# A y-major copy of the queries for the position logits of a two-layer attention kernel

## The chip, the cores and the metric

The kernel runs on one core of one Trainium2 chip. The metric is device time in microseconds (us) of one execution, the median of three runs. The core has a matrix engine (TensorE, PE in the profile; its weight loads are listed apart as PEld), a vector engine (VectorE, DVE), a scalar engine (ScalarE, ACT), a general engine (GpSimd, POOL) and a queue engine that starts transfers (SyncE, SP). Each works through its own instructions in their order and waits for the others through semaphores. Operands lie in on-chip memory of 128 partitions; matmul results go to banks of a separate accumulator memory.

## The reference

The input x has 8 images of 32 x 32 positions with 512 channels. Two layers follow, each of the form x + attention(group norm of x). All arithmetic is float32.

- Layer 0: 16 heads of 32 channels. q, k, v are products of the normed image with one weight matrix; softmax of q k / sqrt(32) over the 1024 positions, times v, then an output projection with a bias.
- Layer 1: 4 heads of 128 channels, three weight matrices for q, k, v and one for the output. Before the softmax a relative position logit is added. For a query at row x and column y and a key at row x' and column y' it is

```
rel_w = einsum('bhxyd,dr->bhxyr', q_w, pos_emb_w)   # entry r picked by y' - y
rel_h = einsum('bhyxd,dr->bhyxr', q_h, pos_emb_h)   # entry r picked by x' - x
scores = attn_q @ k + rel_w + rel_h
```

So for every query column y the queries of that column (all 32 rows, 4 heads) are multiplied with 32 columns of pos_emb_w that depend on y, and for every query row x with 32 columns of pos_emb_h that depend on x.

## The kernel before

Everything of one image is kept channel-major: a block is a tile of 128 partitions (channels of a chunk) by 4 chunks by 1024 positions. The pool has 8 blocks (BLOCKS, line 24). Position n of an image is 32 x + y, so the queries of one row x are 32 adjacent floats and those of one column y are 32 floats apart.

**Products.** Every 512 x 512 projection is done by a Strassen-Winograd scheme of seven products on half matrices, in two units (`seven`, line 417; order of the seven in ORDER, line 181). Each product is a generator step that yields the cost 2 (HC). A unit takes three accumulator banks, x, y and z, from a pool of three ("bank", line 82), which the position logits, and layer 1's scores, use too. ACT copies p1, p7 and the first quarter c11 out of the banks. DVE adds a, b and the quarters c12 and c21. POOL adds the fourth quarter, c22.

**Layer 0's attention** (`attention_0`, line 714) runs through 64 steps per image. A step makes the scores of four heads in a 4-bank tile ps of its own (line 727), lets ACT take the exponential of 128 x 2048 values (line 742, into one of three slots of e_room), multiplies the previous step's exponentials with v (line 753) and lets DVE add them up (line 765).

**Layer 1's attention** (`attention_1`, line 840) adds the position logits by a matmul of posT with a fixed selection matrix (line 851).

**Position logits** (`position_logits`, line 797) are made in four tiles pp per image, each in one bank. A tile holds eight columns y and eight rows x. Line 811 multiplies the queries of one column, line 818 those of one row, each a 128 x 32 weight and 4 x 32 moving columns, on four column strips of the matrix engine. A float32 matmul appears as two records in the trace. From each tile ACT casts four parts of 32 partitions into posT (line 831), rounded to the short matmul format, and DVE writes what the rounding lost into the other partitions (line 836).

**Order.** The program is written by generators. `woven(main, side, start, gap, places)` (line 1151) takes a step of the side after those main steps whose number minus start, modulo gap, is in places. `side_by_side` (line 1163) runs the 64 steps of layer 0's attention of image b and puts beside them, by the yielded costs, all other work: the output projections of earlier images, layer 1's q, k, v and position logits of image b-1 (`second`, line 1083), layer 1's attention of b-1 in one piece (its steps cost 0), and the projections for image b+1. A position tile yields -2, so another product follows before the next attention step. After image 7's layer 0 attention the rest of image 7 runs alone.

A scheduler then orders the instructions of each engine by this program order and by when it expects their operands; `tc.issue_after(ins)` makes what is written inside come after `ins` on its engine. A block or bank is given to a new tile when all users of the old one are done.

In `second`, the q projection runs first, with two sums of the normed image beside it. Then the k projection and the v projection run, 28 products, with the position logits beside them from product 2 on: a tile after products 2, 9, 16 and 23, and its two pairs of differences after the two products that follow.

Of the kernel before, what the change touches and what calls it, by code (L numbers as in the profile page):

```python
# [12 lines left out]
AF = mybir.ActivationFunctionType  # L13
# [14 lines left out]
def quick_path(  # L28
# [23 lines left out]
    nc = tc.nc  # L52

    B, IH, IW, C = x.shape
# [3 lines left out]
    NB = 512  # L58
    NH = N // NB
    D0 = 32  # L60
# [14 lines left out]
    def block(name, shape=None, dtype=F32):  # L75
        return mem.tile(shape or [P, CC, N], dtype, tag="block", name=name, bufs=BLOCKS)

    def chunks(block):
        return [block[:, i, :] for i in range(CC)]
# [51 lines left out]
    HC, HN = CC // 2, NB // 2  # L131
# [49 lines left out]
    ORDER = [0, 5, 1, 4, 6, 2, 3]  # L181
# [151 lines left out]
    beside_norm = [False]  # L333

    added = [None]

    def by_columns(out, weights, moving, start, stop, open_sum=False):

        for g in range(P // 32):
            columns = slice(32 * g, 32 * g + 32)  # L340
            ins = nc.tensor.matmul(  # L341
                out[columns, :],
                weights[:, columns],
                moving,
                start=start,
                stop=stop,
                skip_group_check=open_sum,
            )
            if in_place[0]:
                tc.keep_in_program_order(ins)  # L350
        in_place[0] = False
# [286 lines left out]
    def project_T(fs, m, y, name, units=(0, 1)):  # L638

        for u in units:  # L640
            stream.unit(m, False, u)
            yield from seven(fs, u, False, Plain(halves(y, u)), f"{name}_{u}")
# [71 lines left out]
    def attention_0(q, k, v, b, blocks=range(NT)):  # L714

        steps = [(m, h, j) for m in (0, 2, 1, 3) for h in range(NH) for j in blocks]
        state = {}

        def front(m, h, j):
            name = f"0_{b}_{m}_{h}_{j}"  # L720
            ps = psum.tile([P, HB, NB], F32, tag="ps", name=f"ps_{name}", bufs=1)
            for i in range(2):

                some = slice(64 * i, 64 * i + 64)
                for r in range(HB):
                    rows = slice(r * D0, (r + 1) * D0)
                    nc.tensor.matmul(  # L727
                        ps[some, r, :],
                        k[m][rows, j * P + 64 * i : j * P + 64 * i + 64],
                        q[m][rows, h * NB : (h + 1) * NB],  # L730
                        start=True,
                        stop=True,
                    )
            at = turn.pop(0)
            if j == blocks[0]:

                turn.append(sum_at[0])
                sum_at[0] = at
            else:
                turn.append(at)  # L740
            e = e_room[:, at]
            nc.scalar.activation(e, ps, AF.Exp, scale=D0 ** -0.5)  # L742
            return e

        def back(m, h, j, e):
            name = f"0_{b}_{m}_{h}_{j}"
            if j == blocks[0]:
                state["acc"] = psum.tile([P, NB], F32, tag="acc", name=f"acc_{name}", bufs=1)
                state["first"] = e
            acc = state["acc"]  # L750
            for r in range(HB):
                c0 = (m * HB + r) * D0
                nc.tensor.matmul(  # L753
                    acc[r * D0 : (r + 1) * D0, :],
                    v[:, j, c0 : c0 + D0],
                    e[:, r, :],
                    start=(j == blocks[0]),
                    stop=(j == blocks[-1]),
                )
            if j == blocks[1]:  # L760
                state["esum"] = state["first"]
            if j != blocks[0]:

                with tc.issue_after(reader[0].ins) if beside_norm[0] else nullcontext():
                    summed[0] = nc.vector.tensor_add(state["esum"], state["esum"], e)  # L765
            if j != blocks[-1]:
                return
            nc.scalar.copy(q[m][:, h * NB : (h + 1) * NB], acc)
            state["ended"] = (m, h, state["esum"])

        def finish(m, h, esum):
            name = f"0_{b}_{m}_{h}"
            su = psum.tile([P, NB], F32, tag="acc", name=f"sums_{name}", bufs=1)
            for r in range(HB):
                nc.tensor.matmul(
                    su[r * D0 : (r + 1) * D0, :],
                    ones,
                    esum[:, r, :],
                    start=True,
                    stop=True,  # L780
                )
            normalise(q[m][:, h * NB : (h + 1) * NB], su, name)

        pending = None
        for at in steps:
            if "ended" in state:
                finish(*state.pop("ended"))
            e = front(*at)
            if pending is not None:
                back(*pending)  # L790
            pending = (*at, e)
            yield 2
        back(*pending)
        yield 1
        finish(*state.pop("ended"))

    def position_logits(q, posT, b):

        qv = q.rearrange("p h (x y) -> p h x y", y=IW)
        by_y = posT.rearrange("p h (x s r) -> p r s h x", r=2, s=IW // 2)
        by_x = posT.rearrange("p h (s r y) -> p r s h y", r=2, s=IH // 2)
        G = NB // (IW * H1)
        for t in range(IW // (2 * G)):
            pp = bank(f"pp_{b}_{t}", [P, G, H1, 32])
            for g in range(G):
                for r in range(2):
                    s = 2 * (t * G + g) + r  # L810
                    nc.tensor.matmul(
                        pp[64 * r : 64 * r + 32, g],
                        pw_sb[:, IW - 1 - s : 2 * IW - 1 - s],
                        qv[:, :, :, s],
                        start=True,
                        stop=True,
                    )
                    nc.tensor.matmul(  # L818
                        pp[64 * r + 32 : 64 * r + 64, g],
                        ph_sb[:, IH - 1 - s : 2 * IH - 1 - s],  # L820
                        qv[:, :, s, :],
                        start=True,
                        stop=True,
                    )
            parts = []
            for r in range(2):
                for u, view in enumerate((by_y, by_x)):
                    view = view[:, r, t * G : (t + 1) * G]
                    rows = slice(64 * r + 32 * u, 64 * r + 32 * u + 32)
                    rests = slice(64 * (1 - r) + 32 * u, 64 * (1 - r) + 32 * u + 32)  # L830
                    nc.scalar.copy(view[rows], pp[rows])  # L831
                    parts.append((view[rests], pp[rows], view[rows].bitcast(F32)))

            yield -2
            for i, (rest, logits, greater) in enumerate(parts):
                nc.vector.tensor_sub(rest, logits, greater)  # L836
                if i % 2:
                    yield 0
# [244 lines left out]
    def second(b, st):  # L1083

        if "xn1" in st:
            fs, sums = st.pop("xn1"), st.pop("sums1")
        else:
            fs, sums = forms(st.pop("x1"), f"xn1_{b}"), iter(())
        q = st["ao"] = block(f"q1_{b}")
        yield from woven(project_T(fs, WQ1, chunks(q), f"q1_{b}"), sums, 0, 2 * len(ORDER), (0, 3))  # L1090
        posT = block(f"posT_{b}", dtype=F32R)
        k = chunks(block(f"k1_{b}"))
        v = block(f"v1_{b}", [P, NT, C])
        keys_and_values = chain(
            project_T(fs, WK1, k, f"k1_{b}"), project_rows(fs, WV1, v, f"v1_{b}")
        )

        yield from woven(
            keys_and_values, position_logits(q, posT, b), 2, len(ORDER), (0, 1, 2)
        )  # L1100
        st["at"] = (q, k, v, posT, b)

    def forms_1(b, st):
# [47 lines left out]
    def woven(main, side, start, gap, places=(0,)):  # L1151

        for at, cost in enumerate(main):
            if at >= start and (at - start) % gap in places:
                cost += next(side, 0)
            yield cost
        yield from side
# [21 lines left out]
    def chain(*parts):  # L1179
        for part in parts:  # L1180
            yield from part
# [20 lines left out]
    WP, WQ1, WK1 = Matrix(w_proj, 0, "p"), Matrix(Wq, 0, "q1"), Matrix(Wk, 0, "k1")  # L1202
# [46 lines left out]
    for b in range(B + 1):  # L1249
        rest, total = [], 0  # L1250
        s = [None] * 2 + states + [None] * 2
# [555 lines left out]
```

## Time and profile before

| quantity | value |
|---|---|
| median of three runs | 3792.49 us (3792.39 to 3792.98) |
| profiled execution, its own time | 3792.3 us |
| its span, first to last instruction | 3790.5 us |
| granted clock of the matrix engine | 0.999 |
| position casts, line 831, ACT | 128, 105.7 us busy, mean 826 ns |
| position differences, line 836, DVE | 128, 111.8 us busy, mean 874 ns |
| exponentials of layer 0, line 742, ACT | 512, 961.9 us busy, mean 1879 ns |
| additions of layer 0, line 765, DVE | 448, 1074.6 us busy, mean 2399 ns |

Busy time of a group is the time in which at least one of its instructions runs. The mean of one matmul record is from its start to its last result; the engine begins the next ones long before, so distances between starts tell more than durations. In a timeline a line gives the start, the length, the engine, the source line and the operation, with neighbours of one kind merged (x16: sixteen records). What follows in brackets is how long the engine was idle before and what it waited for. In a table of windows, each engine's busy time in the window is followed by the number of its instructions.

### The profile page before, as it was taken

The page shows a single profiled execution, that of the slowest core. Times are in us where ns is not written, and L with a number is a line of the kernel's source. Part 1 is how long each engine was busy: PE and PEld are TensorE (multiplying, and loading weights), DVE is VectorE, ACT ScalarE, POOL GpSimd, SP SyncE. Part 2 cuts the span into 40 slices and gives each one's busy share as a digit, 9 for nine tenths or more (in the row PEclk, how much of TensorE's full clock was granted, in tenths as well). Part 3 has the DMA queues.
Part 4 walks back from the last instruction along what each step waited for, and adds up shares of the span by engine and source line. Part 5 has one row for each costly group of instructions (what it writes and reads, how often), then busy time and mean ns, then how long its engine had stood idle before and what let it go on. Part 6 is the DMA issues. An engine that isn't in the chain of part 4 may idle for free. (4 is left out here: it accounts for less than half of the span.)

```text
span 3790.5 us, 79715 instructions
## 1 busy us (share of the span) xinstructions
PE 3764.2 (99%) x34478; PEld 1367.7 (36%) x34478; DVE 2579.9 (68%) x2974; ACT 1689.2 (45%) x1705; POOL 651.4 (17%) x397
## 2 busy tenths in 40 slices
PE   9999999999999999999999999999999999999998
PEld 4232244322443234432343323433234332334353
DVE  6778675686756867569665696656866569765555
ACT  3555543445434454344534445344453445553132
POOL 1342101131001310013101131011310113001201
PEclk9999999999999999999999999999999999999999
DMA  6122120232202312023120241103411033110321
GB/s 187 64 106 69 39 57 10 72 102 54 56 12 93 85 48 56 16 92 93 38 56 18 94 96 39 48 22 99 91 40 42 25 99 78 29 43 29 104 50 26
DMA packets 482982, 234.71 MB, mean 62 GB/s; under 512 B 269600, under 2 KB 461376, under 8 KB 481600
## 3 DMA queue, kind: packets, MB, share of 16 engines
q1 hardware_dynamic: 470992, 213.74, 20.6%
q0 software_dynamic: 2608, 13.70, 1.0%
q8 instruction: 273, 4.47, 0.5%
q10 hardware_dynamic: 9024, 2.10, 0.3%
q14 instruction: 85, 0.70, 0.1%
HBM read 170.72 MB, written 58.72 MB: 61 GB/s over the span
## 5 line engine op out<-in xcount | busy, mean ns | idle before, releaser
L765 DVE TENSOR_TENSOR e_room<-e_room 128x2048 f32<-128x2048 f32 x448 | 1074.6, 2399 | 403.3 <-ACT e_room L742 400.1
L742 ACT ACTIVATE e_room<-ps 128x2048 f32<-128x2048 f32 x512 | 961.9, 1879 | 788.6 <-PE ps L727 752.5
L853 ACT ACTIVATE e<-ps 128x512 f32<-128x512 f32 x512 | 306.0, 598 | 634.8 <-PE ps L851 594.2
L727 PE MATMUL ps<-q,k 32*64 32x512 f32 x8192 | 575.5, 613 | 0.2 <-ACT e_room L742 0.2
L753 PE MATMUL acc<-e_room,v 128*32 128x512 f32 x4096 | 551.0, 604 | 0.0
L850 PE MATMUL ps<-q,k 128*128 128x512 f32 x1024 | 529.6, 599 | 0.2 <-DVE posT L836 0.2
L862 PE MATMUL acc<-e,v 128*128 128x512 f32 x1024 | 521.8, 592 | 0.0
L873 DVE TENSOR_TENSOR es<-es,e 128x512 f32<-128x512 f32 x384 | 301.1, 784 | 292.8 <-ACT e L853 288.5
L708 POOL TENSOR_TENSOR q<-q,su 128x512 f32<-128x512 f32 x127 | 190.6, 1501 | 1488.1 <-DVE su L704 1443.6
L851 PE MATMUL ps<-posT,sel 128*128 128x512 f32 x512 | 406.7, 794 | 0.0
L850 PEld LDWEIGHTS ps<-q,k 128*128 128x128 f32 x1024 | 188.2, 190 | 225.1 <-issue 217.3
L727 PEld LDWEIGHTS ps<-q,k 32*64 32x64 f32 x8192 | 120.0, 129 | 389.1 <-issue 216.5
L862 PEld LDWEIGHTS acc<-e,v 128*128 128x128 f32 x1024 | 193.1, 189 | 146.8 <-issue 105.2
L753 PEld LDWEIGHTS acc<-e_room,v 128*32 128x32 f32 x4096 | 81.9, 108 | 411.4 <-issue 364.1
L851 PEld LDWEIGHTS ps<-posT,sel 128*128 128x128 f32 x512 | 97.3, 190 | 122.5 <-issue 122.5
L836 DVE TENSOR_TENSOR posT<-pp,posT 32x512 fp32r<-32x512 f32 x128 | 111.8, 874 | 31.9 <-ACT posT L831 30.6
L593 POOL TENSOR_TENSOR k<-b_k,p_k 128x512 f32<-128x512 f32 x32 | 50.4, 1574 | 478.3 <-ACT p_k L445 467.6
L593 POOL TENSOR_TENSOR v<-b_v,p_v 128x512 f32<-128x512 f32 x32 | 51.5, 1609 | 436.4 <-ACT p_v L445 430.9
L831 ACT CAST posT<-pp 32x512 fp32r<-32x512 f32 x128 | 105.7, 826 | 46.0 <-PE pp L818 44.9
L593 POOL TENSOR_TENSOR q<-b_q,p_q 128x512 f32<-128x512 f32 x32 | 67.6, 2112 | 260.7 <-ACT p_q L445 260.7
L341 PE MATMUL y_v<-w_v,f_xn 128*32 128x256 f32 x1536 | 100.8, 381 | 0.0
L341 PE MATMUL y_k<-f_xn,w_k 128*32 128x512 f32 x768 | 100.7, 594 | 0.0
(223 smaller groups left out, 4384.0 us busy)
## 6 DMA issues: line engine op xcount, KB each, us to landing
w_qkv<-ws_qkv SPq DMA_DIRECT2D x168, 128.0 KB, 2.4
d<-x0T SPq DMA_DIRECT2D x32, 512.0 KB, 3.1
x1T<-d SPq DMA_DIRECT2D x32, 512.0 KB, 5.4
d<-x1T SPq DMA_DIRECT2D x32, 512.0 KB, 3.6
x2T<-d SPq DMA_DIRECT2D x32, 512.0 KB, 6.2
w_qkv<-in_L_conv_w_qkv SPq DMA_DIRECT2D x126, 128.0 KB, 2.2
out<-ot SPq DMA_DIRECT2D x240, 64.0 KB, 2.0
xs<-in_x SPq DMA_DIRECT2D x224, 64.0 KB, 2.5
```

Source lines behind the costliest of these rows:

```text
L341: ins = nc.tensor.matmul(out[columns, :], weights[:, columns], moving, start=start, stop=stop, skip_group_check=open_sum,)
L593: nc.gpsimd.tensor_tensor(self.dst[1][1], s(b), s(p7), op=ALU.add)
L708: engine.tensor_tensor(dst, dst, su, op=ALU.mult)
L727: nc.tensor.matmul(ps[some, r, :], k[m][rows, j * P + 64 * i : j * P + 64 * i + 64], q[m][rows, h * NB : (h + 1) * NB], start=True, stop=True,
L742: nc.scalar.activation(e, ps, AF.Exp, scale=D0 ** -0.5)
L753: nc.tensor.matmul(acc[r * D0 : (r + 1) * D0, :], v[:, j, c0 : c0 + D0], e[:, r, :], start=(j == blocks[0]), stop=(j == blocks[-1]),)
L765: summed[0] = nc.vector.tensor_add(state["esum"], state["esum"], e)
L850: nc.tensor.matmul(ps, k[h][:, keys], q[:, h, queries], start=True, stop=False)
L851: nc.tensor.matmul(ps, sel_flat[:, keys], posT[:, h, queries], start=False, stop=True)
L853: nc.scalar.activation(e, ps, AF.Exp, scale=1.0 / math.sqrt(D1))
L862: nc.tensor.matmul(acc, v[:, j, h * D1 : (h + 1) * D1], e, start=(j == 0), stop=(j == NT - 1),)
L873: added[0] = nc.vector.tensor_add(state["esum"], state["esum"], e)
```

## The change

A second block, turned, holds the queries of an image with the columns outermost: position 32 y + x in place of 32 x + y. Line 811's matmul reads from it, so that the queries of one column are 32 adjacent floats.

`turn_over` makes it with ACT copies of 128 x 512 values, one for each chunk and half, eight per image. The four of a unit's two chunks follow when the unit's products are done: those of unit 0 after products 1 to 4 of unit 1 of the q projection, those of unit 1 after k products 0 to 3. Each is ordered behind the exponential of layer 0 that was written last, which `exps` remembers.

The position steps now follow the last copy: in images 0 to 6 one after every k and v product, from k product 4 on. So the four tiles come after products 4, 7, 10 and 13 of the 28, in place of 2, 9, 16 and 23. In image 7 the tiles stay seven products apart, and come after products 4, 11, 18 and 25. The costs that are yielded are as before.

```diff
+    exps = [None]
...
-            nc.scalar.activation(e, ps, AF.Exp, scale=D0 ** -0.5)
+            exps[0] = nc.scalar.activation(e, ps, AF.Exp, scale=D0 ** -0.5)
...
-    def position_logits(q, posT, b):
+    def position_logits(q, turned, posT, b):
...
+        tv = turned.rearrange("p h (y x) -> p h y x", x=IH)
...
-                        qv[:, :, :, s],
+                        tv[:, :, s, :],
...
-        yield from woven(project_T(fs, WQ1, chunks(q), f"q1_{b}"), sums, 0, 2 * len(ORDER), (0, 3))
+        turned = block(f"turned_{b}")
+
+        def turn_over(u):
+
+            for m in (u, u + HC):
+                for h in range(NH):
+                    with tc.issue_after(exps[0].ins):
+                        nc.scalar.copy(
+                            turned[:, m, :].rearrange("p (y h x) -> p h y x", h=NH, y=IW)[:, h],
+                            q[:, m, h * NB : (h + 1) * NB].rearrange("p (x y) -> p y x", y=IW),
+                        )
+                    yield 0
+
+        def queries(u):
+            return project_T(fs, WQ1, chunks(q), f"q1_{b}", (u,))
+
+        yield from woven(queries(0), sums, 0, len(ORDER), (0, 3))
+        yield from woven(queries(1), turn_over(0), 1, 1)
...
-
-        yield from woven(
-            keys_and_values, position_logits(q, posT, b), 2, len(ORDER), (0, 1, 2)
-        )
+        positions = position_logits(q, turned, posT, b)
+        if b < B - 1:
+            side = woven(keys_and_values, chain(turn_over(1), positions), 0, 1)
+        else:
+            keys_and_values = woven(keys_and_values, turn_over(1), 0, 1)
+            side = woven(keys_and_values, positions, 4, len(ORDER), (0, 1, 2))
+        yield from side
```

## The prediction

> **What bounds the kernel now.** The head of the page comes first:
>
> ```profile
> span 3790.5 us, 79715 instructions
> PE 3764.2 (99%) x34478; PEld 1367.7 (36%) x34478; DVE 2579.9 (68%) x2974; ACT 1689.2 (45%) x1705; POOL 651.4 (17%) x397
> ```
>
> TensorE (PE) leaves 26 us of the span unused, start and end included; no other engine is above 68%. The waits agree on who leads:
>
> ```profile
> engine line waited for: us in total, times, longest us
> ACT e_room L742 <- PE ps L727: 752.5, 489, 4.7
> ```
>
> 489 of the 512 exponentials stand ready for a product that PE has not yet made. So a microsecond off PE is a microsecond off the span, as long as no wait opens elsewhere. Next, the two position matmuls, from the answers for lines 811 and 818 (ns: min/median/max):
>
> ```profile
> L811 PEld LDWEIGHTS pp<-q,pw_sb x512: 110/130/141, 428.3 to 3618.2; 128*32 128x32 f32 x171
> L811 PE MATMUL pp<-q,pw_sb x512: 393/432/451, 428.7 to 3618.4; 128*32 128x128 f32 x171
> L818 PEld LDWEIGHTS pp<-q,ph_sb x512: 106/110/112, 428.3 to 3617.7; 128*32 128x32 f32 x171
> L818 PE MATMUL pp<-q,ph_sb x512: 272/273/299, 428.8 to 3617.9; 128*32 128x128 f32 x171
> ```
>
> Same shapes, same destination bank, same kind of weights. One thing differs: L811 reads the queries in steps of 32 floats, L818 in runs of 32 adjacent ones, and L811 takes 160 ns longer. Last, the timeline around one position tile:
>
> ```profile
> 892.04 1.11 PE L727 MATMUL ps<-q,k 32*64 32x512 f32 x16
> ...
> 897.51 1.11 PE L727 MATMUL ps<-q,k 32*64 32x512 f32 x16
> ...
> 901.15 0.40 PE L811 MATMUL pp<-q,pw_sb 128*32 128x128 f32 x1
> ...
> 901.17 0.38 PE L818 MATMUL pp<-q,ph_sb 128*32 128x128 f32 x3
> ...
> 902.89 0.45 PE L811 MATMUL pp<-q,pw_sb 128*32 128x128 f32 x2
> 903.41 3.34 ACT L831 CAST posT<-pp 32x512 fp32r<-32x512 f32 x4 [1.42 <-PE pp L818]
> 906.71 1.11 PE L727 MATMUL ps<-q,k 32*64 32x512 f32 x16
> 906.79 3.52 DVE L836 TENSOR_TENSOR posT<-pp,posT 32x512 fp32r<-32x512 f32 x4 [0.96 <-ACT posT L831]
> 910.46 1.11 PE L727 MATMUL ps<-q,k 32*64 32x512 f32 x16
> ```
>
> Each L727 line begins an attention step. From 906.71 to 910.46 lie a step and one product (3.75 us), from 892.04 to 897.51 a step and two (5.47): a product is 1.72, a step 2.03. From 897.51 to 906.71 lie a step, three products and one position tile, 9.20: the tile is 9.20 - 2.03 - 5.16 = 2.01 us. It holds eight L811 records on each of two column strips, and their starts run from 901.15 to 902.89: seven gaps of 0.25, and 8 x 0.25 = 2.0. The L818 records on the other two strips need less: a 0.27 record and a group of 0.38 make a gap of 0.11.
>
> **What the Trainium skill says.** "SBUF — State Buffer" (section "Door 1: The DMA port swizzle", the note on cachelines) says that lines are 16 bytes and that each access to a new line pays. L811 touches a new line with every element and the trace agrees: 0.25 against 0.11. "TensorE: Matmul & The Clock Gate" ("Part 3: Packing small matmuls", "The mechanism") says tiles of the array overlap, and loads are pulled ahead of running matmuls; the 0.11 gap of L818, no longer than its own 110 ns load, agrees. "ScalarE: Activation LUTs" ("What ACT_TABLE_LOAD costs") prices an activation with immediates at 186 + 0.833 N ns, an estimate of 612 ns for 512 elements; plain copies here take 586 (L583). The TensorE page ("Architectural detail") also calls ScalarE and VectorE strict FIFOs, which is why order matters below.
>
> **The change, part by part.**
>
> *L811 reads the turned copy.* There are 4 tiles in each of 8 images, 32 in all. The new read is L818's: runs of 32 adjacent floats. A strip then needs 8 x 0.11 = 0.88 us. The bounds: nothing gained if the read is not the cause, and 8 x (0.11 + 0.11) = 1.76 if loads and matmuls don't overlap at that density. I take 0.88, since L818 shows that very gap. Gain 32 x (2.01 - 0.88) = 36.2 us; the pessimistic bound gives 8.
>
> *Eight ACT copies per image, 64 in all.* They read SBUF in steps of 32 floats. No row has ACT reading so; the price lies between 0.59 (plain copy) and 1.07 (L831's strided half, 1.03 to 1.11 us; it writes at such a step). I take 1.07: 68 us, which brings ACT to 46%. On the path they cost nothing as long as they fit: in the tightest gap (3.75) an exponential takes 1.88, the piece 1.07 and one product's copy 0.59, together 3.54. Behind two products (5.47) two pieces fit, 1.88 + 2.14 + 0.59 = 4.61. Queued behind a piece on ACT are the next exponential and product copies p1, p7, c11; the product that needs the exponential's bank comes 0.65 us after it ends in the tightest gap (907.93 + 1.88 to 910.46), so a lateness under that costs nothing. Without this cover the price would be up to 64 x 1.07 = 68 us. What a piece reads was written at least two products earlier, POOL's part (2.1 us) too. The last piece comes behind k product 3; the first position tile follows product 4, 1.72 later.
>
> *One more block.* With q, k, v of the running attention, the normed image, q, posT, k and v of the second layer all 8 blocks are taken. The turned copy is a ninth; but it dies with the last position tile, at k product 13, and v takes its first write behind v product 2. The slot that posT then takes was x2T's, whose last reader (L1123) ends at 855.0 in this image, before all of it. Cost nothing; if positions slipped three products, v would wait.
>
> *Position tiles packed.* They stood 7 products apart; now they follow k products 4, 7, 10 and 13. The pacing sums don't change (each still yields -2), so PE does the same work. But 14.0 us of casts and differences on DVE, and 13.2 on ACT, which lay in some 86 us, now lie in about 33. DVE in the stage before:
>
> ```profile
> 892.00:980.00 88.00, 87.69 (x1164) 34.11 (x1164) 57.92 (x55) 50.49 (x47) 9.57 (x6) 1.00 0.13 39
> ```
>
> Without positions DVE is (57.9 - 14.0)/88 = 50%, so 16.5 in 33; with them 30.5, or 92%. ACT: (50.5 - 13.2)/88 = 42%, 13.9 + 13.2 = 27.1, 82%. Both fit on average, but barely. The banks are the tight part: there are three, and each allocation takes the one of three allocations ago. In the timeline a position bank is held 7.0 us beyond its matmuls: casts to 906.75, then differences to 910.31, which start only when all four casts are done. Working out steps from the costs, tile 0 comes behind k4, then k5, a step, k6, k7, tile 1, and k8 needs tile 0's bank: 3 x 1.72 + 2.03 + 0.88 = 8.07 us after it. Margin 1.07. An e_room addition (2.29) between the two pairs of differences would exceed it by 1.2. Tile 1 needs the bank of the product whose combination (c21, 0.69 on DVE) has one product of time, 1.72; behind a pair of differences (1.75) it is up to 0.8 late. Tiles 2 and 3 stand alike. So four places per image, 0 to about 1.2 each: 0 to 4.6 per image in seven images. I take 1.1, 8 us in all, because PE has some freedom and DVE catches up in between. The last image keeps the spacing, merely two products later: nothing.
>
> *Sum.* 3792.3 (the profiled execution: span 3790.5 and 1.8 around it; 0.2 below the median 3792.49) - 36.2 + 8 = 3764.
>
> **Rivals.**
>
> *Given back.* The bank waits take the upper bound, 4.5 us in each of seven images, 31.5: 3792.3 - 36.2 + 31.5 = 3788. For: DVE at 92% and the three banks. Against: today the same holding of 7 us costs PE nothing.
>
> *Slower.* One mechanism: casts of a packed tile (3.34 us) stand ahead of an exponential on ACT, and the next step's score product, with one bank set of its own, waits for it. The 0.65 cover is spent; a lateness of 3.2 leaves 2.5 at each of 28 tiles, 70 us: 3826. It decides from 36.2/28 = 1.3 us per tile. For: behind tile 1 the step is a 3.75 one, and my walk of ACT puts its exponential there 0.6 late. Against: the other three tiles stand in gaps of 6.3 to 8.1 us.
>
> *It doesn't do what it says.* If the L811 gap came from its weight loads (130 against 110), 3794. Against: loads are short when the strips start alone (110), and 20 ns is not 140.
>
> **How the numbers follow.** Main case 0.71, its own range 3754 to 3778 (no bank waits to 22 us of them). Given back 0.13, from 3779 to 3792. Slower 0.12. No effect 0.04. What can be told from no change here is 0.2%, 7.6 us: faster below 3785. Faster 0.71 + half of given back = 0.78; same 0.06 + 0.04 = 0.10; slower 0.12. The range 3754 to 3790 leaves out the slower case, no effect, and edges of the others.
>
> **What would show it.** Right: L811 near 273 ns, a tile near 0.9 us between its step's marks, 64 new ACT copies of 0.6 to 1.1. PE's idle time grows by under 10 us, before x, y or pp in the k stage. Given back: waits of x, y, pp for DVE of several us per image. Slower: PE waiting before L727 for L742. Wrong altogether: L811 still at 400.

## The result, and the profile after

The changed kernel takes 3783.1 us (median of 12 runs, 3781.0 to 3785.8), the kernel before 3792.6 (3792.3 to 3794.6): a ratio of 0.9975, interval 0.9966 to 0.9984. The gain is 9.5 us where 28 were forecast. The profiled execution took 3782.0, its span is 10.0 us shorter than that of before.

The head of the page of the changed kernel:

```profile
span 3780.5 us, 79769 instructions
PE 3734.0 (99%) x34478; PEld 1340.5 (35%) x34478; DVE 2576.7 (68%) x2974; ACT 1750.4 (46%) x1769; POOL 658.2 (17%) x397
```

PE has 30.2 us less to do, and the span is only 10.0 shorter. So the read did become cheaper, and some 20 us of PE's time turned into waiting. The position matmuls of lines 814 (columns, reading the turned copy) and 821 (rows), in ns as min/median/max:

```profile
L814 PEld LDWEIGHTS pp<-turned,pw_sb x512: 105/110/110, 434.6 to 3607.8; 128*32 128x32 f32 x171
L814 PE MATMUL pp<-turned,pw_sb x512: 270/273/297, 435.0 to 3607.9; 128*32 128x128 f32 x171
L821 PE MATMUL pp<-q,ph_sb x512: 272/273/298, 435.0 to 3607.9; 128*32 128x128 f32 x171
```

The two lines' medians now agree to the nanosecond: 273 where L811 had 432, and the weight loads fell from 130 to 110 as well. The new copies, from the groups by shape (busy us, mean ns, idle before):

```profile
L1100 ACT COPY turned<-q 128x512 f32<-128x512 f32 x64 | 69.7, 1122 | 3.1 <-POOL q L595 2.8 <-DVE q L591 0.2
```

What PE waited for (us in total, times, longest), without the start-up waits that before had too:

```profile
PE y_k L343 <- DVE k L591: 10.6, 6, 2.0
PE y_v L343 <- DVE a_v L433: 5.3, 6, 0.9
...
PE ps L854 <- DVE posT L839: 1.8, 1, 1.8
PE y_v L343 <- DVE v L591: 1.8, 1, 1.8
PE y_v L343 <- DVE k L591: 1.4, 2, 0.8
```

The largest wait for DVE in before was:

```profile
PE y_q L341 <- DVE a_q L431: 0.6, 1, 0.6
```

All that PE waited for DVE adds up to 24.5 us here and to 3.8 in before. DVE computes the differences of the packed tiles. The timeline shows how the first two come about, in the image whose stage before was shown in the prediction:

```profile
905.07 1.90 PE L343 MATMUL y_k<-f_xn,w_k 128*32 128x512 f32 x16
...
908.66 3.53 DVE L839 TENSOR_TENSOR posT<-pp,posT 32x512 fp32r<-32x512 f32 x4 [0.93 <-ACT posT L834]
908.83 1.90 PE L343 MATMUL z_k<-x1T,w_k 128*32 128x512 f32 x16
910.55 1.90 PE L343 MATMUL x_k<-x1T,w_k 128*32 128x512 f32 x16
912.22 2.29 DVE L767 TENSOR_TENSOR e_room<-e_room 128x2048 f32<-128x2048 f32 x1
...
914.54 0.69 DVE L591 TENSOR_TENSOR k<-z_k,a_k 128x512 f32<-128x512 f32 x1
915.28 1.92 PE L343 MATMUL y_k<-f_xn,w_k 128*32 128x512 f32 x16 [1.97 <-DVE k L591]
...
938.03 3.56 DVE L839 TENSOR_TENSOR posT<-pp,posT 32x512 fp32r<-32x512 f32 x4
941.62 2.29 DVE L767 TENSOR_TENSOR e_room<-e_room 128x2048 f32<-128x2048 f32 x1
943.95 0.69 DVE L433 TENSOR_TENSOR a_v<-y_v,p_v 128x512 f32<-128x512 f32 x1
944.70 1.50 PE L343 MATMUL y_v<-w_v,f_xn 128*32 128x256 f32 x24 [0.92 <-DVE a_v L433]
```

Tile 0 ends at 905.07, where the next product starts. The product z_k is complete at 910.73, and its combination c21 (L591, 0.69) would free its bank 0.69 later. But DVE takes its instructions in order, and ahead of c21 stand tile 0's four differences, until 912.19, and one addition of exponentials, until 914.51. So c21 starts 3.8 us after its operand is there, and y_k, which wants that bank, stands still for 1.97 us. At 938 the same happens ahead of a_v, for 0.92. The pair comes in each of images 1 to 5.

Windows of the changed kernel (length; busy time and instructions of PE, PEld, DVE, ACT, POOL; granted clock; DMA share; GB/s): the stretch of the packed tiles, two of the 1.97 us waits with the time behind them, and the k and v products of the last image. Then that last stage in the kernel before.

```profile
905.00:938.10 33.10, 31.14 (x412) 10.38 (x404) 24.18 (x28) 23.52 (x27) 6.07 (x3) 1.00 0.14 41
1843.00:1850.00 7.00, 5.04 (x48) 1.01 (x44) 4.35 (x5) 3.64 (x6) 0.00 (x0) 0.76 0.13 41
2308.00:2316.00 8.00, 6.04 (x91) 1.91 (x85) 5.75 (x6) 4.97 (x6) 0.00 (x0) 1.00 0.19 52
3564.00:3615.00 51.00, 45.87 (x731) 22.86 (x723) 22.70 (x29) 18.96 (x26) 5.11 (x4) 1.00 0.33 102
```

```profile
3566.00:3626.00 60.00, 59.01 (x824) 33.95 (x817) 25.04 (x33) 20.29 (x28) 6.05 (x5) 1.00 0.31 98
```

In the packed stretch DVE is busy 24.18 of 33.1 us, 73%, with the differences of three of the four tiles in it; in the 32.9 us from the first difference to the last (908.66 to 941.60) it is busy 25.95, or 79%. So the wait is not for lack of DVE time. The second and third line hold the same wait of PE; after one of them the granted clock fell, and after the other it did not. In the last image, where attention no longer runs beside, PE is idle 5.1 us of 51 where it was idle 1.0 of 60.

### The profile page after: what moved, and what is told of

Read it like the earlier page. It is cut to its first block, busy times and chain, and to the rows that moved or that the text cites. A ratio compares the mean times of both kernels' runs of the same rounds, so it can differ in the third digit from the quotient of the medians.

```text
span 3780.5 us, 79769 instructions
## 1 busy us (share of the span) xinstructions
PE 3734.0 (99%) x34478; PEld 1340.5 (35%) x34478; DVE 2576.7 (68%) x2974; ACT 1750.4 (46%) x1769; POOL 658.2 (17%) x397
## 4 chain that ended last, share of the span: by engine, by line
PE 87%; DVE 8%; issue 2%; ACT 1%; POOL 1%; DMA 0%; SPq 0%; DVEq 0%; ACTq 0%; POOLq 0%
PE ps L729 12%; PE ps L853 12%; PE acc L865 12%; PE acc L755 11%; PE y_v L343 4%; PE y_q L343 4%; PE y_k L343 4%; DVE e_room L767 3%; PE ps L854 3%; PE z_v L343 3%; PE z_q L343 3%; PE x_q L343 3%; PE x_k L343 2%; PE x_v L343 2%; PE y_wp L343 2%
## 5 line engine op out<-in xcount | busy, mean ns | idle before, releaser
L729 PE MATMUL ps<-q,k 32*64 32x512 f32 x8192 | 576.4, 613 | 0.6 <-ACT e_room L744 0.6
L854 PE MATMUL ps<-posT,sel 128*128 128x512 f32 x512 | 407.1, 795 | 1.8 <-DVE posT L839 1.8
L729 PEld LDWEIGHTS ps<-q,k 32*64 32x64 f32 x8192 | 120.1, 130 | 386.9 <-issue 200.1
L854 PEld LDWEIGHTS ps<-posT,sel 128*128 128x128 f32 x512 | 97.4, 190 | 125.1 <-issue 125.1
L343 PE MATMUL y_k<-f_xn,w_k 128*32 128x512 f32 x768 | 91.8, 595 | 10.6 <-DVE k L591 10.6
L343 PE MATMUL y_v<-w_v,f_xn 128*32 128x256 f32 x1536 | 91.9, 380 | 8.4 <-DVE a_v L433 5.3
```

What stands on the lines that cost most here:

```text
L343: ins = nc.tensor.matmul(out[columns, :], weights[:, columns], moving, start=start, stop=stop, skip_group_check=open_sum,)
L729: nc.tensor.matmul(ps[some, r, :], k[m][rows, j * P + 64 * i : j * P + 64 * i + 64], q[m][rows, h * NB : (h + 1) * NB], start=True, stop=True,
L854: nc.tensor.matmul(ps, sel_flat[:, keys], posT[:, h, queries], start=False, stop=True)
```

## The experiments

Medians in us; the ratio is against the kernel before on the same chip, with its 95% interval.

| run | what it is | time | ratio |
|---|---|---|---|
| e1_read | before, cheap read | 3757.5 | 0.9907 (0.9891 to 0.9922) |
| e2_copies | before, with block and copies | 3794.5 | 1.0004 (0.9996 to 1.0012) |
| e3_packed | before, tiles packed | 3809.4 | 1.0043 (1.0029 to 1.0057) |
| e4_nocopies | after, no block, no copies | 3781.4 | 0.9968 (0.9956 to 0.9980) |
| e5_nodiff | after, differences off DVE | 3757.8 | 0.9907 (0.9891 to 0.9924) |
| e6_gap3 | after, tiles one product earlier | 3779.5 | 0.9965 (0.9952 to 0.9977) |
| f2_gap4 | after, four products apart | 3778.1 | 0.9962 (0.9948 to 0.9976) |
| f5_last | after, last image one product earlier | 3784.0 | 0.9976 (0.9967 to 0.9986) |
| e7_late_add | after, additions behind c21 | 3773.3 | 0.9944 (0.9931 to 0.9958) |
| f6_jit | before, turned per tile, 2 copies | 3820.9 | 1.0069 (1.0055 to 1.0083) |
| f7_jit1 | before, turned per tile, 1 copy | 3825.0 | 1.0084 (1.0070 to 1.0098) |
| f8_rows | before, turned per tile in existing tiles | 3761.9 | 0.9917 (0.9904 to 0.9931) |

### One part at a time: e1 to e4

**e1_read** takes the kernel before and only makes line 811 read runs of 32 adjacent floats. The column logits are then computed from the queries of rows.

```diff
-                        qv[:, :, :, s],
+                        qv[:, :, s, :],
```

> The kernel before with one edit: the column matmul reads the queries by rows, in runs of 32 adjacent floats, as its neighbour does. No copies, no ninth block, tiles at their old places; the column logits are then those of the rows, so part of the computation is changed. Theory A (reading was the cost, and what was lost came from packing the tiles): each of 32 tiles falls from 2.01 to 0.88 us with no new wait, 3792.6 - 36.2 = 3756, between 3753 and 3762. Rival B (shorter tiles alone make PE wait, since ACT and DVE cannot follow): 3770 to 3785.

Measured: 3757.5, 35.3 us below before. Its line 811:

```profile
L811 PE MATMUL pp<-q,pw_sb x512: 272/273/273, 429.3 to 3583.6; 128*32 128x128 f32 x171
```

Nothing but the operand's step (and with it the values) changed, and 432 ns became 273. The step is the cause, and it is worth 35.3 us of the end-to-end time when nothing else moves: 1.10 per tile, against the 1.13 of the prediction.

**e2_copies** is the changed kernel with its block and its 64 copies, but line 817 reads q as before, and the tiles stand after products 2, 9, 16 and 23.

```diff
-                        tv[:, :, s, :],
+                        qv[:, :, :, s],
...
-        if b < B - 1:
-            side = woven(keys_and_values, chain(turn_over(1), positions), 0, 1)
-        else:
-            keys_and_values = woven(keys_and_values, turn_over(1), 0, 1)
-            side = woven(keys_and_values, positions, 4, len(ORDER), (0, 1, 2))
-        yield from side
+        keys_and_values = woven(keys_and_values, turn_over(1), 0, 1)
+        yield from woven(keys_and_values, positions, 2, len(ORDER), (0, 1, 2))
```

> The changed kernel with the copies kept, but nobody reads them: the column matmul reads q again, and the tiles stand at their old places (after k and v products 2, 9, 16, 23). Theory A (copies are hidden on ACT): within 4 us of the kernel before, 3789 to 3797. Rival C (the 70 us of ACT copies or the ninth block cost the time that is missing): 3805 to 3820.

Measured: 3794.5, 1.8 above before, with an interval that holds 1. In its profile the excess lies mostly at the ends: 5.1 us before the first matmul and 11.5 behind the last, where before has 4.7 and 10.0. PE's gaps between matmuls add up to 11.9, in before to 11.6. So 70 us of new work on ACT cost next to nothing. Nobody reads the copy here, so its block comes free after the last copy; what the block costs with readers is left to e4.

**e3_packed** is the kernel before with its slow reads and no copies; only the tiles stand where the changed kernel has them.

```diff
-        yield from woven(
-            keys_and_values, position_logits(q, posT, b), 2, len(ORDER), (0, 1, 2)
-        )
+        positions = position_logits(q, posT, b)
+        if b < B - 1:
+            side = woven(keys_and_values, positions, 4, 1)
+        else:
+            side = woven(keys_and_values, positions, 4, len(ORDER), (0, 1, 2))
+        yield from side
```

> The kernel before with only the places of the tiles changed: after k and v products 4, 7, 10 and 13 in images 0 to 6, after 4, 11, 18, 25 in image 7; slow reads, no copies. Theory A (packing makes PE wait for banks that DVE frees late): slower than before, but by less than the waits in the changed kernel, since each tile is 1.13 us longer and the wait behind it that much shorter: about 1 us per image and 4 in the last, 3799 to 3806. Rival C: 3790 to 3795, packing costs nothing.

Measured: 3809.4, 16.7 above before, more than expected. Two of its waits of PE:

```profile
PE y_k L341 <- DVE k L589: 5.1, 6, 0.9
PE y_v L341 <- DVE a_v L431: 5.1, 6, 0.9
```

The packing alone makes the two waits, without copies and without the fast read. With the slow read the one at y_k is 0.9; with the fast read it is 1.97. A tile that is 1.1 us shorter brings PE to the bank 1.1 us earlier, and DVE frees it no sooner. Part of what the read gains in these tiles is thus lost at once.

**e4_nocopies** is the changed kernel without block and copies; line 817 reads the rows of q, so it has the cheap read and the packed tiles.

```diff
-                        tv[:, :, s, :],
+                        qv[:, :, s, :],
...
-        turned = block(f"turned_{b}")
+        turned = None
...
```

> The changed kernel without the copies and without the block turned: the column matmul reads q by rows (so the column logits are changed), tiles packed as in the change. Theory A: the time of the changed kernel within 4 us, 3779 to 3787, with the same waits of about 2 and 0.9 us per image. Rival C (copies or block cost it): 3756 to 3768.

Measured: 3781.4, 24.0 above e1. It lies 1.7 below the changed kernel, which its own spread (3777.7 to 3785.3) doesn't resolve. The parts are thus: read -35.3, packing with the fast read +24.0, copies and block +1.7 here or +1.8 in e2. That is -9.5, the measured gain; the sum closes because these last two agree, and is no check beyond that.

### What the packing waits for: e5

**e5_nodiff** is the changed kernel with its tiles packed, but the 128 differences are not computed on DVE; POOL fills their places with zeros.

```diff
-                nc.vector.tensor_sub(rest, logits, greater)
+                nc.gpsimd.memset(rest.bitcast(F32), 0.0)
```

> The changed kernel with the position differences taken off DVE: where DVE wrote what the rounding lost, POOL writes zeroes (that part of the computation is left out). Theory A (PE waits for banks whose release stands behind the differences on DVE): the waits before y products in the k and v stage vanish, and with them nearly all of what is missing: 3754 to 3764. Rival D (the casts on ACT, ahead of exponentials and of p1 copies, are what holds PE): 3774 to 3784, the waits stay.

Measured: 3757.8, the same as e1. The longest that is left of the k stage's waits for DVE:

```profile
PE y_k L343 <- DVE k L591: 1.0, 5, 0.2
```

With casts, copies and packed matmuls all in place, the whole cost of the packing goes away with the differences. The casts and copies on ACT, which the rival of a slower kernel had in mind, cost nothing by themselves. But the edit does two things: it takes work off DVE, and it lets a position bank go as soon as its casts have read it.

### Phase, density or order: e6, f2, f5 and e7

That differences on DVE do it leaves open how. They could fall at a bad place among the seven products, they could be too many in too short a time, or they could stand in the wrong place of DVE's strict order.

**e6_gap3** moves the tiles of images 0 to 6 to products 3, 6, 9 and 12 (in image 7 to 3, 10, 17 and 24); the last four copies are put at products 0 (two), 1 and 2.

```diff
...
+        keys_and_values = woven(keys_and_values, turn_over(1, 2), 0, 1)
+        gap = 3 if b < B - 1 else len(ORDER)
+        yield from woven(keys_and_values, positions, 3, gap, (0, 1, 2))
```

> The changed kernel with each tile one product earlier (after products 3, 6, 9, 12; copies after k products 0, 0, 1, 2; image 7 after 3, 10, 17, 24): same density, other phase against the seven products. If the density alone makes PE wait (DVE 92% busy): 3776 to 3786. If the phase does it (a combination whose bank the second unit needs stands right behind four differences and an addition): 3762 to 3773.

Measured: 3779.5, 3.6 below the changed kernel. The phase theory, which wanted 3762 to 3773, missed. The waits say why:

```profile
PE y_v L343 <- DVE a_v L433: 4.0, 6, 0.7
...
PE y_k L343 <- DVE k L591: 2.9, 5, 0.6
```

The 1.97 us wait is down to 0.6, as hoped, but the other stays at 0.7, and PE waits 4.9 us for ACT besides, at the scores of layer 0 and at acc.

**f2_gap4** has the same edit with a gap of 4: tiles after products 3, 7, 11 and 15.

> The changed kernel with the tiles four products apart in images 0 to 6 (after 3, 7, 11, 15; copies after k products 0, 0, 1, 2), and after 3, 10, 17, 24 in image 7. Theory A: DVE has 11.7 in place of about 8.2 us for a tile, PE waits well under 1 us per image: 3757 to 3768. Rival D: 3774 to 3784.

Measured: 3778.1. A third more time for the same differences brings 1.4 us against e6, from which it differs in the spacing alone, and 5 us against the changed kernel, of the 24. So the density theory, which wanted 3757 to 3768, missed as well. In both kernels image 7 is part of the reason, which the next run takes alone.

**f5_last** is the changed kernel; only image 7's tiles move, to products 3, 10, 17 and 24.

```diff
...
-            keys_and_values = woven(keys_and_values, turn_over(1), 0, 1)
-            side = woven(keys_and_values, positions, 4, len(ORDER), (0, 1, 2))
+            keys_and_values = woven(keys_and_values, turn_over(1, 2), 0, 1)
+            side = woven(keys_and_values, positions, 3, len(ORDER), (0, 1, 2))
```

> The changed kernel with image 7 alone altered: its tiles come after products 3, 10, 17, 24 in place of 4, 11, 18, 25, so that the tile takes its bank before z does, as in the kernel before. Theory A: the four waits of 0.8 to 1.8 us in image 7 fall to 0.2 to 0.3 each, 3 to 6 us in all: 3777 to 3781. Rival D: no difference, 3781 to 3786.

Measured: 3784.0, no gain where 3777 to 3781 was expected. In image 7 the four waits for DVE of 0.8, 0.8, 1.8 and 1.8 us turned into four of 1.0 to 1.1: two for another combination (L588), two for the differences themselves. Four new ones of 0.6 came on top, at z, for copies that ACT makes behind the tile's casts. That is 6.4 us in place of 5.1. Moving a tile by a product only chooses what stands behind its casts and differences. With the first tile at product 2, as in before, the longest wait of this stage was 0.3 us.

**e7_late_add** leaves every tile where the changed kernel has it and takes no work away. Only DVE's order is altered: in the k products the addition of a step's exponentials is held back until the last c21 has been issued.

```diff
+    owed, postponed, gate = [], [False], [None]
...
-            nc.vector.tensor_add(self.dst[0][1], self.shape(z), self.shape(a))
+            gate[0] = nc.vector.tensor_add(self.dst[0][1], self.shape(z), self.shape(a))
...
-                with tc.issue_after(reader[0].ins) if beside_norm[0] else nullcontext():
-                    summed[0] = nc.vector.tensor_add(state["esum"], state["esum"], e)
+                def add(esum=state["esum"]):
+                    first = reader[0] if beside_norm[0] else gate[0] if postponed[0] else None
+                    with tc.issue_after(first.ins) if first is not None else nullcontext():
+                        summed[0] = nc.vector.tensor_add(esum, esum, e)
+                owed.append(add)
+                if not postponed[0] or j == blocks[-1]:
+                    settle()
...
```

> The changed kernel with all its work and all its tiles where they are; only in the k products the addition of a step's two halves of exponentials is put behind the last combination of the c21 products (k of x1), so that VectorE does the tile's four differences, then k of x1, then the additions, then a_k. Order theory (the strict order of VectorE holds back the bank that the next k product needs): TensorE's wait of about 2 us at a product y_k, once in each of images 0 to 6, falls below 0.5, the waits of about 0.9 at y_v and those of the last image stay, and the time is 3770 to 3777. Fullness theory (VectorE simply has too much to do while the tiles are packed, whatever the order): the wait only moves to the next product, and the time stays at 3780 to 3787.

Measured: 3773.3, 9.8 below the changed kernel, as the order theory expected. The same place in its timeline, which here lies 3.8 us later:

```profile
912.44 3.54 DVE L852 TENSOR_TENSOR posT<-pp,posT 32x512 fp32r<-32x512 f32 x4 [0.93 <-ACT posT L847]
...
916.01 0.69 DVE L592 TENSOR_TENSOR k<-z_k,a_k 128x512 f32<-128x512 f32 x1
...
916.62 4.68 DVE L770 TENSOR_TENSOR e_room<-e_room 128x2048 f32<-128x2048 f32 x2
916.93 1.90 PE L344 MATMUL y_k<-f_xn,w_k 128*32 128x512 f32 x16
```

Here c21 follows the differences directly, the additions come behind it, and y_k starts without a wait. What e7 did not reorder stayed as it was, and one wait is new:

```profile
PE y_v L344 <- DVE a_v L434: 5.3, 6, 0.9
...
PE pp L827 <- DVE posT L852: 1.8, 1, 1.8
```

So of the 24.0 us, 9.8 are shown to come from DVE's order alone, from an addition that stands ahead of one combination. That this equals five waits of 1.97 is chance: PE's gaps fell by 7.6 us only (31.3 to 23.7), since a tile in image 0 now waits 1.8 for the differences before it; the other 2.2 are not assigned. The waits at y_v (5.3) and three of the four in the last image have the same look in the timeline, a combination behind a tile's differences, but no run altered their order alone. The fourth there, 1.8 us, is another thing: layer 1's attention (L854) waits for the last tile's differences themselves.

### Turning the queries just ahead of each tile: f6, f7 and f8

If the spacing is what counts, the tiles should stay seven products apart, with the turned queries made in quarters. **f6_jit** does so from the kernel before: two ACT copies of 128x512 at products 0 and 1, the tile at 2, and so on every seven products. A quarter lies in a tile of 4 KB per partition, whose room comes from the weight tiles, 12 in place of 16.

```diff
-                    t = mem.tile([P, HN], F32, tag="w", name=f"w_{m.name}_{n}_{i}_{c}", bufs=16)
+                    t = mem.tile([P, HN], F32, tag="w", name=f"w_{m.name}_{n}_{i}_{c}", bufs=12)
...
+            tv = mem.tile([P, H1, 2 * G, IH], F32, tag="turn", name=f"turn_{b}_{t}", bufs=1)
+            for u in range(0, H1, 2):
+                with tc.issue_after(exps[0].ins):
+                    nc.scalar.copy(
+                        tv[:, u : u + 2].rearrange("p h y x -> p h x y"),
+                        qv[:, u : u + 2, :, 2 * t * G : 2 * (t + 1) * G],
+                    )
+                yield 0
...
```

> The kernel before with its spacing kept (tiles after k and v products 2, 9, 16, 23), and the queries turned over a quarter at a time, just ahead of each tile: two ACT copies of 128x512 values after the two products before it, into one 4 KB tile in place of a block (room from the weight tiles, 12 in place of 16). Theory A (the read is worth 36 us, copies are hidden, the waits come from packing, and packing came from the ninth block): 3756 to 3764. Rival E (copies ahead of a tile make it late, or 12 weight tiles are too few): 3766 to 3785.

Measured: 3820.9, slower than before by 28, where 3756 to 3764 was hoped for. The reason is not in the tiles:

```profile
PE z_v L343 <- DMA w_qkv<-ws_qkv: 30.0, 7, 19.5
```

PE waits for weights, up to 19.5 us at once. With 12 tiles their loads start too late: f8 below, which keeps 16, has no such wait. **f7_jit1** differs by one ACT copy of 128x1024 per tile in place of two halves:

> As the run with quarters, but one ACT copy of 128x1024 values per tile, after the product before the tile's last: half the instructions, about 2.1 us each in one piece. Theory A: 3756 to 3764. If a long copy makes exponentials late: 3764 to 3775.

Measured: 3825.0, with the same 12 weight tiles; it says nothing for one copy or two.

**f8_rows** keeps the 16 weight tiles and all 8 blocks. Each half of a quarter goes into one of the three 2 KB tiles into which the rows of the next image's input are loaded, and which stand empty in this stage. Those loads are ordered behind the last weight load instead.

```diff
-                    nc.sync.dma_start(t, src[:, c, :])
+                    fed[0] = nc.sync.dma_start(t, src[:, c, :])
...
+            tv = []
+            for u in range(2):
+                tv.append(mem.tile([P, H1, G, IH], F32, tag="row", name=f"turn_{b}_{t}_{u}", bufs=3))
+                s0 = (2 * t + u) * G
+                with tc.issue_after(exps[0].ins):
+                    nc.scalar.copy(
+                        tv[u].rearrange("p h y x -> p h x y"), qv[:, :, :, s0 : s0 + G]
+                    )
+                yield 0
...
-                        qv[:, :, :, s],
+                        tv[s // G - 2 * t][:, :, s % G, :],
...
-        with tc.issue_after(put[0].ins) if b == 1 else nullcontext():
+        with tc.issue_after(put[0].ins if b == 1 else fed[0].ins):
...
-            keys_and_values, position_logits(q, posT, b), 2, len(ORDER), (0, 1, 2)
+            keys_and_values, position_logits(q, posT, b), 0, len(ORDER), tuple(range(5))
```

> The kernel before with its spacing kept (tiles after k and v products 2, 9, 16, 23); the queries of a tile are turned over just ahead of it by two ACT copies of 128x512 values, after the two products before it, into two of the three 2 KB tiles that the loading of rows uses (idle in this stage; the loads of the next image are ordered behind the weight loads for it). All 16 weight tiles and 8 blocks stay. Theory A (read worth 36 us, copies hidden, waits from packing, weights were what failed in the run with quarters): 3756 to 3766. Rival E (the copies just ahead of a tile make it or its users late): 3770 to 3785.

Measured: 3761.9, 21.2 below the changed kernel and 31.0 below before. It lies within 4.5 us of e1, which makes no copies at all. PE's gaps add up to 16.2 us where before has 11.6, and 4.4 of the 16.2 lie in the k and v products of image 7. What f8 loses to e1 lies there: from the start of image 6's layer 1 attention to that of image 7 it takes 286.5 us, e1 282.1.

## Where the prediction was right, and where it failed

- **The bound and the price of the read: right.** PE sets the end. The gap of L818 was the right price for L811: 0.87 us per tile where 0.88 was taken, 35.3 us of time where 36.2 was forecast. The Trainium skill's note on 16-byte lines in "SBUF — State Buffer" ("Door 1: The DMA port swizzle"), which that step rested on, agrees with e1, where the step of the operand is all that changed; no run varies the step, so the width of a line is not tested.
- **Eight copies per image: right within 2 us.** 1.12 us each where 1.07 was taken; with some luck, since that was the price of a write in steps. They cost 1.7 to 1.8 us at most where none was forecast (e2, e4), which the noise doesn't set apart from nothing.
- **One more block: right**, within the same 1.7 us (e4).
- **Position tiles packed: this step failed.** "I take 1.1, 8 us in all" measured 24.0 (e4 less e1). Three things in it were wrong. The step set the tight bank as tile 0's, with a margin of 1.07; in the trace tile 1 took that bank, 0.07 us after the last difference, just without a wait, and the late bank was that of the product z_k (in the prediction tile 1 wants it, in the trace the product behind tile 1). For a combination behind position work it let c21 stand "behind a pair of differences (1.75)", up to 0.8 late; four differences and an addition stood ahead, 3.53 + 2.29, and 1.97 us of waiting came of it. And it let "DVE catches up in between" soften the sum; DVE had the time (79% busy over the four tiles where 92% was feared) but not the order. Both engine shares in that step were beside the point. The strict order of ACT and DVE was named in the prediction, but only ACT's queue was walked through; for DVE single lines were set against single banks. So PE's idle time, which was to grow by under 10 us, grew by 19.7, in images 1 to 5 at two places of 1.97 and 0.9 where four of up to 1.2 were set.
- **The last image: wrong too.** "Merely two products later: nothing" was 5.1 us of waits where before had 1.0: three combinations stand behind differences, and the last tile comes so late that attention waits for it. The layer 1 attention of the last image starts 286.9 us after that of the image before it, in before 286.7: the 4.5 us that the read should have gained there are gone.
- **What no step held: the clock.** In the profiled execution two of the waits were followed by a spell of half clock, 1.6 us each, told below.

**The rivals.** "Given back" is what happened, and at a size close to its own: 3788 was worked out from 4.5 us of bank waits in each of seven images, and the cost found is 24.0 in all. That nearness is partly luck: the waits are 2.9 us in each of images 1 to 5, and 5.1 in the last image, where the rival had none. Its argument against, that 7 us of holding cost nothing today, was true only for tiles with nothing urgent behind them. "Slower" did not come: PE waited 0.6 us in all for exponentials before L729. "It doesn't do what it says" is refuted by e1: the step alone took matmuls and weight loads down together.

The sum, changed kernel less before, from the two profiles (PE's idle time is the sum of all gaps between the end of one matmul and the start of the next):

| term | us |
|---|---|
| busy time of PE: cheap read, as in e1's profile | -35.6 |
| busy time of PE: two spells of half clock, 1.56 and 1.57 | +3.1 |
| busy time of PE: rest, cause open | +2.3 |
| idle time of PE: 31.3 in after, 11.6 in before | +19.7 |
| before the first and behind the last matmul | +0.5 |
| sum: change of the span | -10.0 |

The medians differ by 9.5. The copies have no line of their own: what e2's profile shows of them lies in the stretches at both ends, 16.6 us there, 15.3 in after and 14.7 in before.

## What to carry to other kernels

A share of busy time says whether an engine can do the work, not whether it does it in time: where work is moved or packed, list each in-order engine's instructions around it, find the one that frees the next bank, and add up all that stands ahead of it. An operand's price can be read from a neighbour of the same shape, and a separate run of the read alone (e1) shows what there is to win before its preparation is built. Prepare it in small pieces in room that is idle anyway, so that nothing else has to move: that took 31.0 us off (f8), and the same read with the tiles packed took 9.5.

## What was not expected of the hardware

- **Some waits of about 2 us were followed by half clock.** In image 3, PE waited from 1843.33 to 1845.29. The time behind it (PE, PEld, DVE, ACT, POOL; granted clock; DMA share; GB/s):

```profile
1846.00:1847.00 1.00, 1.00 (x12) 0.13 (x4) 0.00 (x0) 0.67 (x2) 0.00 (x0) 0.81 0.00 0
1847.00:1848.00 1.00, 1.00 (x12) 0.33 (x16) 0.19 (x1) 0.00 (x0) 0.00 (x0) 0.50 0.00 0
1848.00:1849.00 1.00, 1.00 (x16) 0.00 (x0) 0.97 (x2) 0.00 (x0) 0.00 (x0) 0.50 0.15 50
1849.00:1850.00 1.00, 1.00 (x12) 0.20 (x8) 0.99 (x2) 0.29 (x1) 0.00 (x0) 0.50 0.26 89
1850.00:1851.00 1.00, 1.00 (x12) 0.24 (x8) 0.99 (x2) 1.00 (x1) 0.00 (x0) 0.98 0.00 0
```

From the end of this wait to the one at y_v lie 30.06 us where image 1 has 28.50. In the last image the wait of 1.82 us was followed by the same, and the attention from its first to its last L854 took 124.94 where before took 123.37. The other five waits of this length in that profile had no such sequel. Past the first 30 us, the profiles of after, e3, e4, e6, e7 and f5 hold 25 waits of 1.7 to 2.0 us. A spell followed 9 of them within 1.4 us, and none came elsewhere before the last matmul. The profiles of before, e1, e2, e5, f2 and f8 hold no such wait and no spell up to their last matmul; f6 and f7, which have longer waits, are left out. e4's profile has four spells, and is the slowest of its six executions (3785.3; the fastest 3777.7). The skill ("TensorE: Matmul & The Clock Gate", "What's actually happening") has half clock as the state after an idle window of about 3.4 us, and the same page's "Why this matters for your kernels" advises against gaps above about 3 us. Here the spells last 3.4 us by the clock shown, but gaps of 1.8 to 2.0 us were enough for some of them. This was only seen: no run made waits of chosen lengths.
- **ACT's price for steps of 32 floats.** The casts of 512 values per partition (before, L831) took 0.58 us where they write runs of 32 adjacent floats and 1.03 to 1.11 where they write in steps. The turning copies, 128x512 values read in steps, took 1.12 (1.14 in f8), plain copies of that size out of the accumulators 0.59. No copy here reads the on-chip memory without a step, so what the step of a read costs is not separated from what the source costs.
- **Four fewer weight tiles of sixteen** came with 40 us of waits for weights in f6, one of 19.5 us.
